# Four-layer graph network on one core: layer 0 with loads two chunks further ahead, its range sums stored from ScalarE's queue into four tables

## The chip, the cores and the metric

The kernel runs on one core of a Trainium2 chip. A core has five engines with instruction queues of their own, TensorE (PE in the profile), VectorE (DVE), ScalarE (ACT), GpSimd (POOL) and SyncE (SP), and sixteen DMA engines that they share. The metric is the device time of one execution in microseconds (us), as the median of several runs without a profiler. The profile is of one further execution.

## What is computed

Four message-passing layers over the same 400,000 edges and 12,500 nodes with 32 features. The edges are sorted by their destination. Every layer starts with a layer normalisation and a relu and adds its result to x:

```python
h = jnp.maximum(_layernorm(x, axis=-1), 0.0)
x = x + _L0_gnn_ref(h, edge_attr_32, L0_gnn_eps, src, dst)
...
def _L0_gnn_ref(node_feat, edge_feat, eps, src, dst):
    m = jax.nn.relu(node_feat[src] + edge_feat)
    neigh = jax.ops.segment_sum(m, dst, num_segments=node_feat.shape[0])
    return (1.0 + eps[0]) * node_feat + neigh
```

Layer 0 thus gathers a row of 32 numbers for each edge, adds that edge's own 32 numbers, applies a relu, and sums by destination. Layers 1 to 3 are of the same form with more work on each edge. Layer 2 needs the degree of each node, the number of edges that leave from it by src; the kernel counts that in layer 0.

## The kernel before

**Tiling.** The edges lie in 128 partitions by 3136 columns (padded). A chunk is 16 columns, 2048 edges; there are 196 chunks. A chunk is worked on in four groups of four columns. Because the edges are sorted by destination, the destinations of a chunk lie in a range of at most 128 nodes; a check at the start confirms that and chooses this "fast" form of all layers.

**The loop.** `edges` (L471 on) is used by layer 0 with all 196 chunks written out in one pass. It runs four groups ahead (`AHEAD`): for group g it fetches group g+4, does the main part of g, and the tail of g-1. The first fetch of a chunk also loads the chunk: `src` (L427, 8 KB), `edge_attr` (L425, 256 KB) and `local` (L408, which holds each edge's place in the chunk's range and, in a last column, the start row of the range). All three are issued by SP, from a pool `big0` of two buffers each. The planner of the framework may move instructions within an engine by its own priorities; it keeps what depends on what.

**A group.** GpSimd issues four indirect DMAs (L433), one for each column, that gather 128 rows of the node features into `hs`; the pool has six `hs` buffers. VectorE adds the edges' numbers (m, L560), ScalarE applies the relu (L561; three m buffers). In the tail, `collect` (L376) makes a one-hot tile `oh` on VectorE (L382) and TensorE adds the messages into the chunk's range in PSUM, `ps_win` (L385). Then the degree count: four small instructions on VectorE for `hi` and `lo` (L575 to L578), two one-hot tiles `ohi` and `olo` (L582), and a product on TensorE into `ps_deg` (L585).

**The end of a chunk.** ScalarE copies `ps_win` to `wsum` (L388, two buffers), and `put` stores that to a table in DRAM from SP's queue (L398), at the start row that SP reads from `local` (L402). Ranges of neighbouring chunks may overlap, so even chunks store to one table and odd ones to another. VectorE adds `ps_deg` to the degrees (L588).

**Before the loop and beside it.** `rest` (L196) is a generator that prepares things: it fills a tile with zeros (L201), clears the tables of all layers with it from ScalarE's queue (`clear`, L313 and L314; 1.6 MB for a table and a small tail), then loads weights and computes unit vectors for later layers. Two steps of it, the two tables of layer 0, are taken before the loop, the others beside its groups.

**After the loop.** `gather_sum` (L363) reads the tables back, by turns on the queues of SP and ScalarE (L369), and VectorE adds them (L372). Then come x and the next layer's normalisation, which everything in layer 1 waits for. Layers 1 and 3 also use two tables, layer 2 four.

**What holds an instruction back.** Each engine takes its instructions in order. A DMA issued by an engine waits, at the head of that engine's queue, for the tiles that it reads or overwrites, and for the transfer that used the same completion semaphore last; eight of these go round over the DMAs of SP and ScalarE. Whatever stands behind it on that engine waits too.

Of the kernel before, what the change touches and what calls it, by code (L numbers as in the profile page):

```python
# [8 lines left out]
F32 = mybir.dt.float32  # L9
# [7 lines left out]
P = 128  # L17
D = 32
# [3 lines left out]
CPI0 = 7  # L22
CPI1 = 196
AHEAD = 4
Q4 = 4
B = G * CG * P // Q4
NTAB = 4
ROUND = 12582912.0

TANH_GAIN = 1.593  # L30
# [5 lines left out]
class GNN:  # L36
# [94 lines left out]
    def weights(self, pool):  # L131
# [19 lines left out]
        nc.vector.memset(hid, 0.0)  # L151
        for q in range(Q4):
            nc.sync.dma_start(hid[32 * q : 32 * q + 10], self.a["w1t"])
# [43 lines left out]
    def rest(self, pool):  # L197

        nc, J = self.nc, self.J
        zero = pool.tile([P, J * D], F32, name="zero")  # L200
        nc.vector.memset(zero, 0.0)  # L201
        for l in range(4):
            for t in self.tabs[l][:2] if self.fast and l != 2 else self.tabs[l]:
                self.clear(t, zero)
                yield
        yield from self.weights(pool)
        if self.fast:
            yield from self.places_by_edge(pool)
            yield from self.unit_vectors(pool)
# [153 lines left out]
    def gather_sum(self, l, pool):  # L363

        nc = self.nc
        parts = []
        for k, t in enumerate(self.tabs[l][: 2 if self.fast and l != 2 else NTAB]):
            s = pool.tile([NP, self.J, D], F32, name=f"part{k}")
            (nc.sync, nc.scalar)[k % 2].dma_start(s.rearrange("p j d -> p (j d)"), self.nodes(t[: self.N]))  # L369
            parts.append(s)  # L370
        for part in parts[1:]:
            nc.vector.tensor_add(parts[0], parts[0], part)  # L372
        return parts[0]


    def collect(self, l, pool, psum, c, feat, t0):  # L376

        nc = self.nc
        if t0 == 0:
            c["sum"] = psum.tile([P, D], F32, name="ps_win")  # L380
        oh = pool.tile([P, G, P], F32, name="oh")
        nc.vector.tensor_tensor(oh, self.iota[:, None, :].to_broadcast([P, G, P]),  # L382
                                c["local"][:, t0 : t0 + G, None].to_broadcast([P, G, P]), op=ALU.is_equal)
        for k in range(G):
            nc.tensor.matmul(c["sum"], lhsT=oh[:, k, :], rhs=feat[:, k, :], start=t0 + k == 0, stop=t0 + k == self.CT - 1)  # L385
        if t0 + G == self.CT:
            s = pool.tile([P, D], F32, name="wsum")
            nc.scalar.copy(s, c["sum"])  # L388
            self.put(l, c, s)

    def get(self, pool, l, c):

# [3 lines left out]
    def put(self, l, c, s):  # L396

        self.nc.sync.dma_start(self.tabs[l][c["no"] % 2][ds(self.first(c), P), :], s)  # L398

    def first(self, c):  # L400
        if "first" not in c:
# [70 lines left out]
    def edges(self, load, gather, front, main, tail, begin=None, windowed=None, beside=None):  # L472


        CPI = CPI1 if self.fast else CPI0
        IT = self.CT * CPI
        with self.tc.For_i(0, self.T // IT, 1) as it:
            i = it * IT
            n = CPI * CG
            chunks, state = {}, {}  # L480
            whole = begin(i) if begin else None

            def fetch(g):
                c, k = divmod(g, CG)
                if k == 0:
                    chunks[c] = load(i + c * self.CT)
                    if whole is not None:
                        chunks[c] |= {x: t[:, c * self.CT : (c + 1) * self.CT] for x, t in whole.items()}
                    chunks[c]["no"] = c
                    if windowed:  # L490
                        windowed(chunks[c], it * CPI + c)
                state[g] = (chunks[c], k * G, gather(chunks[c], k * G))

            def ahead(g):
                state[g] += (front(*state[g]),)

            for g in range(AHEAD):
                fetch(g)
            ahead(0)
            for g in range(n):  # L500
                if g + AHEAD < n:
                    fetch(g + AHEAD)
                if g + 1 < n:
                    ahead(g + 1)
                state[g] = state[g][:2] + (main(*state[g]),)
                if g:
                    tail(*state.pop(g - 1))
                if beside and g > 4 * CG and g % 2:
                    next(beside, None)
            tail(*state.pop(n - 1))  # L510
            for _ in beside or ():
                pass
# [10 lines left out]
    def layer0(self):  # L523
        nc, tc, J = self.nc, self.tc, self.J
# [4 lines left out]
        with ExitStack() as ctx:  # L529
            rest = None  # L530
            if self.fast:
                rest = self.rest(ctx.enter_context(tc.tile_pool(name="rest", bufs=1)))
                for _ in range(2):
                    next(rest)
            big = ctx.enter_context(tc.tile_pool(name="big0", bufs=2))
            gp = ctx.enter_context(tc.tile_pool(name="gather0", bufs=AHEAD + 2))
            wp = ctx.enter_context(tc.tile_pool(name="work0", bufs=2))
            psum = ctx.enter_context(tc.tile_pool(name="psum0", bufs=2, space=PSUM))
            hist = ctx.enter_context(tc.tile_pool(name="hist0", bufs=2, space=PSUM))

            def load(col):
                if self.fast:
                    c = {n: self.load(big, n, col) for n in ("src", "edge_attr_32")}
                else:
                    c = {n: self.load(big, n, col) for n in ("src", "dst", "edge_attr_32")}
                    c["row"] = self.load_row(big, "dst_t", col)
                    c["rows"] = big.tile([P, self.CT], I32, name="rows")
                c["col"] = col
                c["deg"] = hist.tile([P, P], F32, name="ps_deg")
                return c  # L550

            def gather(c, t0):
                return self.gather(gp, "hs", 0, c["src"], t0)

            def front(c, t0, hs):
                return None

            def main(c, t0, hs, _):
                m = wp.tile([P, G, D], F32, name="m", bufs=3)
                nc.vector.tensor_add(m, hs, c["edge_attr_32"][:, t0 : t0 + G, :])  # L560
                nc.scalar.activation(m, m, AF.Relu)  # L561
                return m

            def tail(c, t0, m):
                if self.fast:
                    self.collect(0, wp, psum, c, m, t0)
                else:
                    eq = self.same(wp, c["dst"], c["row"], t0)
                    self.firsts(wp, eq, c["dst"], c["rows"], t0)
                    self.scatter(0, wp, psum, eq, m, c["rows"], t0)  # L570

                hi = wp.tile([P, G], F32, name="hi")
                lo = wp.tile([P, G], F32, name="lo")
                s = c["src"][:, t0 : t0 + G]
                nc.vector.tensor_scalar(hi, s, -0.5 * (J - 1), 1.0 / J, op0=ALU.add, op1=ALU.mult)  # L575
                nc.vector.tensor_scalar_add(hi, hi, ROUND)
                nc.vector.tensor_scalar_add(hi, hi, -ROUND)
                nc.vector.scalar_tensor_tensor(lo, hi, -float(J), s, op0=ALU.mult, op1=ALU.add)  # L578
                ohi = wp.tile([P, G, NP], BF16, name="ohi")
                olo = wp.tile([P, G, J], BF16, name="olo")  # L580
                for oh, v, n in ((ohi, hi, NP), (olo, lo, J)):
                    nc.vector.tensor_tensor(oh, self.iota[:, None, :n].to_broadcast([P, G, n]),  # L582
                                            v[:, :, None].to_broadcast([P, G, n]), op=ALU.is_equal)
                for k in range(G):
                    nc.tensor.matmul(c["deg"][:NP, :J], lhsT=ohi[:, k, :], rhs=olo[:, k, :],  # L585
                                     start=t0 + k == 0, stop=t0 + k == self.CT - 1)
                if t0 + G == self.CT:
                    nc.vector.tensor_add(self.deg, self.deg, c["deg"][:NP, :J])  # L588
                    if not self.fast:
                        nc.scalar.dma_start(self.dst_rows[:, ds(c["col"], self.CT)], c["rows"])  # L590

            self.edges(load, gather, front, main, tail,
                       windowed=(lambda c, row: c.update(self.places_of(big, row))) if self.fast else None, beside=rest)
        with tc.tile_pool(name="end0", bufs=1) as pool:
# [794 lines left out]
```

## Time and profile before

| | us |
|---|---|
| time, median of 3 runs | 19167.42 (19167.29 to 19172.29) |
| the profiled execution | 23109.4 |
| its span in the trace | 23107.7 |
| in it: start, up to the first gather of layer 0 | 0 to 85 |
| layer 0's loop | 85 to 5027 |
| sum of its tables, x, normalisation | 5027 to 5105 |
| layers 1 and 2 | 5105 to 16280 |
| layer 2's end and normalisation | to 16330 |
| layer 3 | 16330 to 23107 |

The profiled execution is longer than the others, so a duration in it is compared with durations in it, and a change of the time with the median.

Layer 0 in the profiled execution, 85 to 5027 us:

| engine | busy us | instructions |
|---|---|---|
| PE | 1831.8 | 9408 |
| DVE | 1975.7 | 6649 |
| ACT | 277.5 | 994 |
| POOL | 3136.3 | 3136 |

A line of groups shows busy time, mean time of one in ns, and the idle time just before such instructions with what ended most of it. A waits line shows who waited for what: the sum, how many times, the longest. A timeline line shows start, length, engine, line and operation; SPq and ACTq are DMA issues on the queues of SP and ScalarE.

### The profile page before, as it was taken

Reading aid. Unit: us, or ns where it says so; the run is one execution under the profiler, and the core shown is the slowest. Engines: PE = TensorE matmul, PEld = TensorE weight load, DVE = VectorE, ACT = ScalarE, POOL = GpSimd, SP = SyncE. Lnnn points to the kernel's source line nnn. Section 1 sums busy time; section 2 is a strip of 40 time slices with the busy share of each in tenths; the row PEclk is TensorE's granted clock in tenths of the full one; section 3 lists DMA queues with packets and bytes.
Section 4 is the critical chain, followed back from the end, with each engine's and each line's share of the span. In section 5 each row is a group of like instructions: output and inputs, shape, how many; then the busy total and the mean of one; then the engine's idle time right before and its main releaser. Section 6 shows DMA issues by size and latency. Waiting matters only on the chain.

```text
span 23107.7 us, 229565 instructions
## 1 busy us (share of the span) xinstructions
PE 15954.9 (69%) x74484; PEld 8493.8 (37%) x74484; DVE 11868.8 (51%) x24410; ACT 5515.5 (24%) x12954; POOL 14407.0 (62%) x12552
## 2 busy tenths in 40 slices
PE   2333333328888778778777777787588888888887
PEld 2333333322333333333333333333355445445544
DVE  4443333335555555555555555555455555555555
ACT  0000000002222222222222222222233333333333
POOL 5666666655777777777777777777444444444443
PEclk9999999998777777777777777777687888888887
DMA  2111111113333333333333333333100000000000
GB/s 74 42 35 23 23 23 23 23 40 73 80 80 79 77 78 83 77 78 82 80 78 81 80 77 79 78 83 77 24 12 12 12 12 12 12 12 12 12 12 18
DMA packets 1503407, 1138.52 MB, mean 49 GB/s; under 512 B 1141492, under 2 KB 1304900, under 8 KB 1448308
## 3 DMA queue, kind: packets, MB, share of 16 engines
q1 hardware_dynamic: 745098, 891.46, 12.3%
q0 software_dynamic: 752640, 206.32, 9.7%
q10 hardware_dynamic: 4448, 25.89, 0.3%
q8 instruction: 592, 9.70, 0.2%
q14 instruction: 629, 5.15, 0.1%
HBM read 1022.56 MB, written 99.86 MB: 49 GB/s over the span
## 4 chain that ended last, share of the span: by engine, by line
PE 39%; DVE 18%; another core or an unknown queue 15%; issue 11%; ACT 9%; POOL 5%; DMA 2%; DVEq 0%; SPq 0%; POOLq 0%; ACTq 0%
PE ps_y L746 11%; PE ps_w L1162 10%; PE ps_o L756 4%; PE ps L879 4%; ACT oh L781 3%; DVE z L749 3%; DVE rb L1180 3%; POOL hs L433 2%; DVE pb L1172 2%; PE ps_h L1140 2%; ACT oh L710 2%; PE ps_win L385 2%; PE ps_sum L1201 1%; DVE f L1178 1%
## 5 line engine op out<-in xcount | busy, mean ns | idle before, releaser
L885 POOL DMA_INDIRECT acc<-summed,rows x3136 | 4995.6, 1593 | 1898.0 <-issue 1141.3
L1130 POOL DMA_INDIRECT hs<-feat,src x3136 | 3085.0, 984 | 3653.4 <-DVE pb L1172 2657.8
L1162 PE MATMUL ps_w<-w2b,hid 128*128 128x256 f32 x12544 | 4006.1, 462 | 608.6 <-issue 430.0
L433 POOL DMA_INDIRECT hs<-feat,src x3136 | 3136.5, 1000 | 1881.0 <-issue 864.2
L704 POOL DMA_INDIRECT hs<-feat,src_c x3136 | 3189.0, 1017 | 1126.7 <-issue 932.0
L1162 PEld LDWEIGHTS ps_w<-w2b,hid 128*128 128x128 f32 x12544 | 2722.3, 227 | 2283.9 <-issue 1572.6
L749 DVE TENSOR_TENSOR z<-ps_y,hid 128x1024 f32<-128x1024 f32 x2352 | 2842.0, 1218 | 1235.5 <-PE ps_y L746 1007.3
L385 PE MATMUL ps_win<-m,oh 128*128 128x32 f32 x6272 | 1488.0, 402 | 2521.3 <-ACT m L561 1829.8
L746 PE MATMUL ps_y<-X,w2t 64*128 64x512 f32 x4704 | 2258.9, 838 | 613.4 <-ACT hid L741 306.4
L385 PEld LDWEIGHTS ps_win<-m,oh 128*128 128x128 f32 x6272 | 1398.1, 328 | 2612.4 <-ACT m L561 1921.6
L1167 DVE TENSOR_TENSOR pa<-ps_w,q 128x512 f32<-128x512 f32 x784 | 536.0, 684 | 3153.4 <-PE ps_w L1162 2928.4
L756 PE MATMUL ps_o<-z,sums 128*32 128x512 f32 x9408 | 1936.9, 697 | 2.5 <-issue 1.6
L746 PE MATMUL ps_y<-Q,w2t 64*128 64x512 f32 x4704 | 1688.5, 740 | 83.6 <-DVE z L749 39.8
L723 PE MATMUL ps_m<-eye,hs 128*32 128x128 f32 x6272 | 805.2, 367 | 1048.3 <-ACT X L729 790.5
L879 PEld LDWEIGHTS ps<-hd,eq 128*128 128x128 f32 x6272 | 1048.0, 253 | 1241.9 <-issue 339.4
L879 PE MATMUL ps<-hd,eq 128*128 128x32 f32 x6272 | 1144.2, 335 | 513.7 <-DVE eq L871 197.1
L732 DVE TENSOR_TENSOR Q<-N,X 128x512 f32<-128x512 f32 x392 | 271.6, 693 | 2115.6 <-ACT X L729 1473.0
L1142 ACT ACTIVATE hid<-ps_h 128x1024 f32<-128x1024 f32 x784 | 799.8, 1020 | 2236.2 <-PE ps_h L1140 1651.5
L1172 DVE TENSOR_TENSOR pb<-ps_w,hs 128x256 f32<-128x256 f32 x3136 | 1281.8, 469 | 0.0
L1140 PE MATMUL ps_h<-emb,w1q 8*128 8x512 f32 x3136 | 1066.5, 761 | 230.0 <-DMA emb<-in_ea_c 165.1
L746 PEld LDWEIGHTS ps_y<-X,w2t 64*128 64x128 f32 x4704 | 603.4, 236 | 1658.0 <-issue 742.6
L723 PEld LDWEIGHTS ps_m<-eye,hs 128*32 128x32 f32 x6272 | 546.2, 147 | 1635.2 <-ACT X L729 929.7
(191 smaller groups left out, 18563.7 us busy)
## 6 DMA issues: line engine op xcount, KB each, us to landing
has<-loc_t SPq DMA_DIRECT2D x392, 1024.0 KB
srow<-in_src_t SPq DMA_DIRECT2D x392, 512.0 KB
hs<-feat,src POOLq DMA_INDIRECT x6272
N<-n_t SPq DMA_DIRECT2D x3136, 32.0 KB
edge_attr<-in_edge_attr SPq DMA_DIRECT2D x196, 256.0 KB
hs<-feat,src_c POOLq DMA_INDIRECT x3136
acc<-summed,rows POOLq DMA_INDIRECT x3136
emb<-in_ea_c SPq DMA_DIRECT2D x784, 20.0 KB
```

The source lines that it names most:

```text
L385: nc.tensor.matmul(c["sum"], lhsT=oh[:, k, :], rhs=feat[:, k, :], start=t0 + k == 0, stop=t0 + k == self.CT - 1)
L433: self.nc.gpsimd.indirect_dma_start(out=t[:, k, :], out_offset=None, in_=self.feats[l][:], in_offset=bass.IndirectOffsetOnAxis(ap=idx[:, t ...
L704: nc.gpsimd.indirect_dma_start(out=c["hs"][:, k, :], out_offset=None, in_=self.feats[1][:], in_offset=bass.IndirectOffsetOnAxis(ap=c["src_ ...
L746: nc.tensor.matmul(y[:, q, :], lhsT=self.w2t[64 * q : 64 * q + 64, j, :], rhs=c["Q" if j < 3 else "X"][64 * q : 64 * q + 64, h, :], start= ...
L749: nc.vector.tensor_mul(z, y, c["hid"][:, 2 * h : 2 * h + 2, :])
L756: nc.tensor.matmul(c["o", j // 3][32 * q : 32 * q + 32, :], lhsT=self.sums[:, j, :], rhs=c["z", j, q // 2][:, q % 2, :], start=j % 3 == 0, ...
L879: nc.tensor.matmul(t[:, k, :], lhsT=c["eq"][:, k, :], rhs=c["hd"][:, G * g + k, :], start=True, stop=True)
L885: nc.gpsimd.indirect_dma_start(out=self.tabs[2][k % NTAB][:], out_offset=bass.IndirectOffsetOnAxis(ap=c["rows"][:, G * g + k : G * g + k + ...
L1130: nc.gpsimd.indirect_dma_start(out=c["hs"][:, k, :], out_offset=None, in_=self.feats[3][:], in_offset=bass.IndirectOffsetOnAxis(ap=c["src" ...
L1140: nc.tensor.matmul(t[:, q, :], lhsT=self.w1q[r : r + 8, m * P : (m + 1) * P], rhs=c["emb"][r : r + 8], start=True, stop=True)
L1162: nc.tensor.matmul(w[:, k, :], lhsT=c["hid"][:, m, 4 * g + k].rearrange("p q s -> p (q s)"), rhs=self.w2b[:, m, :], start=m == 0, stop=m == 1)
L1172: nc.vector.tensor_mul(c["pb"][:, i, gs], w[:, :, lo : lo + 64].rearrange("p g (w u) -> p g w u", u=8), by[:, :, None, :].to_broadcast([P, ...
```

## The change

Layer 0's chunks are asked for two chunks earlier: when the first group of chunk c is fetched, everything up to chunk c+2 that is not yet asked for is loaded (`LEAD`), and `big0` has six buffers instead of two. Its range sums go to four tables by turns instead of two, from four `wsum` buffers instead of two; the start row is read and the store issued on ScalarE's queue instead of SP's (`put_late`). `TABS` says how many tables each layer has; so four tables of layer 0 are cleared ahead of the loop, and four are read and added behind it. The PSUM tile of the degrees is asked for at the chunk's first tail instead of with its loads. Layers 1 to 3 keep their numbers of tables, and the other users of `put` keep it.

```diff
+LEAD = 2
+TABS = {0: 4, 1: 2, 2: 4, 3: 2}
...
-            for t in self.tabs[l][:2] if self.fast and l != 2 else self.tabs[l]:
+            for t in self.tabs[l][: TABS[l]] if self.fast else self.tabs[l]:
                 self.clear(t, zero)
                 yield
...
-        for k, t in enumerate(self.tabs[l][: 2 if self.fast and l != 2 else NTAB]):
+        for k, t in enumerate(self.tabs[l][: TABS[l] if self.fast else NTAB]):
...
         if t0 + G == self.CT:
-            s = pool.tile([P, D], F32, name="wsum")
+            s = pool.tile([P, D], F32, name="wsum", bufs=4)
             nc.scalar.copy(s, c["sum"])
-            self.put(l, c, s)
+            self.put_late(l, c, s)
...
+    def put_late(self, l, c, s):
+
+        first = self.nc.values_load(c["wbase"], engines=[mybir.EngineType.Activation], min_val=0, max_val=self.N - 1)
+        self.nc.scalar.dma_start(self.tabs[l][c["no"] % TABS[l]][ds(first, P), :], s)
...
                 if k == 0:
-                    chunks[c] = load(i + c * self.CT)
-                    if whole is not None:
-                        chunks[c] |= {x: t[:, c * self.CT : (c + 1) * self.CT] for x, t in whole.items()}
-                    chunks[c]["no"] = c
-                    if windowed:
-                        windowed(chunks[c], it * CPI + c)
+                    for c1 in range(len(chunks), min(c + 1 + (LEAD if self.fast else 0), CPI)):
+                        chunks[c1] = load(i + c1 * self.CT)
+                        if whole is not None:
+                            chunks[c1] |= {x: t[:, c1 * self.CT : (c1 + 1) * self.CT] for x, t in whole.items()}
+                        chunks[c1]["no"] = c1
+                        if windowed:
+                            windowed(chunks[c1], it * CPI + c1)
...
-                for _ in range(2):
+                for _ in range(TABS[0]):
                     next(rest)
-            big = ctx.enter_context(tc.tile_pool(name="big0", bufs=2))
+            big = ctx.enter_context(tc.tile_pool(name="big0", bufs=LEAD + 4 if self.fast else 2))
...
-                c["deg"] = hist.tile([P, P], F32, name="ps_deg")
...
+                if t0 == 0:
+                    c["deg"] = hist.tile([P, P], F32, name="ps_deg")
```

## The prediction

> **What bounds the kernel now.** I read the page first, then busy time by stretch, then the waits of layer 0, then the instructions of one pair of chunks, and last the start and the end of layer 0.
>
> From the page (busy us, mean ns of one | idle before, main releaser), and the chain's shares:
>
> ```profile
> span 23107.7 us, 229565 instructions
> ...
> PE 39%; DVE 18%; another core or an unknown queue 15%; issue 11%; ACT 9%; POOL 5%; DMA 2%; DVEq 0%; SPq 0%; POOLq 0%; ACTq 0%
> ...
> L433 POOL DMA_INDIRECT hs<-feat,src x3136 | 3136.5, 1000 | 1881.0 <-issue 864.2
> ```
>
> The profiled execution took 23109.4 us, 3942 us more than the median of 19167.4. Layers 1 to 3 lie after 5027 us, and the change leaves their instructions and order alone but for a few at the border. So only layer 0, 85 to 5027 us, is in play, plus what stands just before and behind it. There POOL issues 3136 gathers, 16 a chunk. One takes 0.94 us and 0.30 us of issue, so a chunk costs 16 x 1.25 = 20.0 us on POOL.
>
> Busy time in four stretches of 500 us (columns: stretch, PE, PEld, DVE, ACT, POOL, clock, DMA share, GB/s):
>
> ```profile
> 500.00:1000.00 500.00, 182.07 (x918) 174.59 (x918) 235.28 (x702) 29.68 (x102) 316.53 (x308) 1.00 0.16 38
> 1500.00:2000.00 500.00, 189.11 (x972) 179.18 (x970) 200.38 (x675) 28.23 (x102) 321.23 (x322) 1.00 0.12 25
> 4000.00:4500.00 500.00, 185.69 (x960) 175.93 (x960) 188.65 (x663) 27.71 (x101) 317.87 (x322) 1.00 0.11 23
> ```
>
> No engine is full. POOL makes 308 to 322 gathers in each stretch, 25 us a chunk instead of 20, and the rate hardly moves while VectorE's load falls from 235 to 189 us. So 5 us a chunk are lost to a wait. The waits of POOL from 2000 to 5000 us (us in total, times, longest):
>
> ```profile
> POOL hs L433 <- issue: 520.7, 1703, 2.1
> POOL hs L433 <- DVE oh L382: 313.4, 35, 14.5
> POOL hs L433 <- DMA src<-in_src: 150.5, 22, 9.4
> ```
>
> One pair of chunks, from the timeline:
>
> ```profile
> 2088.13 0.19 ACT L388 COPY wsum<-ps_win 128x32 f32<-128x32 f32 x1 [22.32 <-remote]
> ...
> 2088.34 0.34 SPq L398 DMA_DIRECT2D acc<-wsum  x1
> 2089.63 0.33 SPq L427 DMA_DIRECT2D src<-in_src  x1
> ...
> 2091.97 0.94 POOL L433 DMA_INDIRECT hs<-feat,src  x1 [7.72 <-DVE oh L382]
> ...
> 2098.43 0.34 SPq L398 DMA_DIRECT2D acc<-wsum  x1
> 2104.79 0.33 SPq L427 DMA_DIRECT2D src<-in_src  x1
> ```
>
> The copy of the range sum waits 22.3 us for a release that the trace can't name. The store of that sum (L398) stands on SP ahead of the next chunk's load of src (L427), so both come late and POOL starts 2.3 us after src is issued. In the next chunk nothing is late: src goes out at 2104.79, while that chunk's 17th gather after 2091.97, the first to need it, is at 2113.40. With 2.3 us for landing, src was 6.3 us early. So the order on SP costs nothing by itself. It costs only when the range sum is late, every second chunk, and what makes it late is the unnamed wait.
>
> **What the Trainium skill says.** "Perfetto Trace Analysis", section "Tensor Engine Instruction (MATMUL, LD_WEIGHTS)", has a matmul's end in a profile as an estimate. So the unnamed 22 us may be TensorE reporting late: matmuls look ended and their results are not released. The trace agrees that far, and does not say whether that happens without the profiler. "DMA: Bandwidth & Descriptors", "Issuing engines are not separate DMA queues", says that transfers of SP and ScalarE run on the same 16 DMA engines; its section "Why a DMA increments its semaphore by 16 and not by 1" splits a transfer over the largest number up to 16 that divides the partitions, five for 125. The trace agrees: two reads of 125x3200 float32, one on each queue, took 26.6 us together, four took 52 (below), so a second queue bought nothing.
>
> **The change, part by part.**
>
> *End: two more tables to sum.* Layer 2 of this kernel already sums four:
>
> ```profile
> 16224.84 14.84 SPq L369 DMA_DIRECT2D part<-acc  x2
> ...
> 16276.84 3.49 DVE L372 TENSOR_TENSOR part<-part,part 125x3200 f32<-125x3200 f32 x1 [0.34 <-DMA part<-acc]
> ```
>
> and layer 0 two:
>
> ```profile
> 5027.16 0.34 SPq L369 DMA_DIRECT2D part<-acc  x1
> ...
> 5053.73 3.49 DVE L372 TENSOR_TENSOR part<-part,part 125x3200 f32<-125x3200 f32 x1 [25.31 <-DMA part<-acc]
> ```
>
> From the first read to the end of the last add: 16280.33 - 16224.84 = 55.5 us against 5057.22 - 5027.16 = 30.1. That is +25.4 us. Of the two added adds (3.49 us each) one or both lie under transfers; if neither did, +29. VectorE waits for nothing else there and layer 1 can't start, so all of it is on the path. I take 25.4, ends 22 and 30.
>
> *Start: two more tables to clear.* The waits of SP at the start, and POOL's first gather and its only long wait for src before 300 us:
>
> ```profile
> SPq L425 <- DMA acc<-zero: 12.2, 1, 12.2
> SPq L408 <- DMA acc<-zero: 9.7, 1, 9.7
> ...
> 84.81 1.47 POOL L433 DMA_INDIRECT hs<-feat,src  x1 [82.96 <-DVE lo L578]
> ...
> POOL hs L433 <- DMA src<-in_src: 14.4, 1, 14.4
> ```
>
> The two waits end at 84.1 and 97.0 us: a clear of 1.6 MB lands every 12.9 us, and loads that share its completion semaphore wait for it. In the changed order four clears stand ahead of the first load. By the instruction order its src waits for the first clear's tail (84.2), the second chunk's src for the third clear (110). With 3 to 9 us to land, the first gather moves from 84.8 to 88 to 94 (+3 to +9), and the second chunk, due 20 us later, waits 2 to 8 more: +5 to +17. Against this stands the 14.4 us wait at the third chunk, whose src came at 130 us behind weight loads on SP. Six chunks are now asked for ahead of the weights, so it goes. Net -9 to +3; I take -2. Three later waits for src (9.3 us from 300 to 1000) go too, some of them into waits for buffers: -4.
>
> *Steady state: loads ahead, and the store on ScalarE's queue.* SP loses per chunk the store (0.34 us) and the reading of its start row (0.95 us between the store's issue and src's at 2089.63); ScalarE gains them, 1.3 us in 20. ScalarE is busy 277.5 of 4942 us in layer 0, and behind the store wait the relus of groups 5 us apart, so this hides; if a relu of each chunk were late by all of it with no slack behind, 196 x 1.3 = 255 us. I take 0: three m and six hs buffers stand between that relu and POOL. The store waits for TensorE (through the copy) as before; queued behind it are now the relus, which also stood behind the copy, and no longer src, local and edge_attr. Four wsum buffers and four tables lengthen the distance between writes to one place; no wait on them shows in the trace, so nothing. The degree tile asked for at the chunk's first tail leaves TensorE's sequence of four and four matmuls as it was.
>
> What the loads ahead save in the middle hangs on the unnamed wait. If it belongs to profiled executions, POOL runs without it at 20 to 21 us a chunk, src is 6 us early, and they save nothing. For this: 15% of the chain, 3466 us, are "unknown", and 3942 us are missing in the runs without a profile. In layer 0 POOL's waits beyond issue are 1881.0 - 864.2 = 1017 us, about a quarter of the missing time, for a stage with a fifth of the span. Against: nothing shows where the missing time lies. I take the saving as 0, ends -208 (all waits for src in layer 0, as the page's trace sums them) and -1017.
>
> Sum, against the profile's own time: +25.4 - 2 - 4 = +19 us, 23109 to 23128, less whatever of the src waits goes there. None of the three terms is a TensorE matter, so I carry them over to the median unchanged: 19167.4 + 19 = 19,186 us.
>
> **Rivals.** Forecast: no measurable change (0.2% of this kernel, 38 us, is what a measurement can tell). The two extra tables eat about what the loads ahead save at the start.
>
> Rival one, faster: the late range sums are real in every execution. Then SP's order stops POOL in every second chunk or so and src, now two chunks ahead, does not. With the waits for src gone and the tables paid: 19167 + 25 - 208 = 18,985. For it: the pair above, where POOL starts 2.3 us after src. Against: from 300 to 1000 us only 9.3 us of src waits, yet the same rate of gathers; there POOL waits for hs buffers held by the same late TensorE, so src waits may only be renamed, and the gain goes towards 0. If POOL's whole idle time went, 19167 + 25 - 1017 = 18,175, the far end.
>
> Rival two, slower: the start is not repaid. Place: ScalarE's queue before 140 us. In the changed order the reading of two start rows stands there ahead of the first relu, and the second row's load waits for the fourth clear, 68 + 16 + 3 x 12.9 = 123 us. The first relu, at 99.9 now, comes at about 125. Six hs groups hold 30 us of gathers from about 90, three m tiles some 15 more. It decides if POOL is stopped by more than about 15 us net; stopped by the full 25, with the 14.4 us saved elsewhere in part, the time is 19167 + 25 + 25 = 19,217.
>
> **How the numbers follow.** No change 0.38; rival one 0.30, and 0.03 for more than that; rival two 0.25, and 0.04 for the store on ScalarE showing (up to 19,440). So faster 0.33, same 0.38, slower 0.29. The forecast's own range is 19,150 to 19,205. To leave out no more than 2 in 10 the range must take rival one to a little below its time and rival two to above it: 18,930 to 19,260.
>
> **What would show it.** Right: first gather at 88 to 94 us; no POOL wait for src after 300 us; the part sum from first read to last add 52 to 60 us; ScalarE's store beside relus that still follow VectorE; layers 1 to 3 as long as before. The steady state is wrong if the median falls below 19,130, the start if the first 16 gathers show waits for hs buffers of over 15 us, ScalarE's share if relus wait for its queue. A profiled layer 0 that is much shorter while the median stays would show that the unnamed wait is the profile's.

## The result and the profile after

The changed kernel takes 19194.3 us in the median of 20 runs (19183.6 to 19214.1), the kernel before, beside it, 19168.0 (19144.5 to 19190.3). The ratio is 1.0015, with an interval of 1.0009 to 1.0022: slower by 17 to 42 us. Most of that interval lies below the 38 us that the prediction called measurable. 19,186 had been forecast.

The page of the changed kernel, the lines that answer to the first ones of before:

```profile
span 19191.0 us, 229975 instructions
...
PE 40%; POOL 22%; DMA 13%; issue 8%; DVE 8%; ACT 8%; another core or an unknown queue 0%; DVEq 0%; POOLq 0%; ACTq 0%; SPq 0%
...
L440 POOL DMA_INDIRECT hs<-feat,src x3136 | 3170.6, 1011 | 1052.0 <-issue 777.1
```

The profiled execution now lasts as long as the others, and the unnamed 15% of the chain are gone. That is no merit of the change: a new profile of the kernel before has none of them either (experiment 1). The first one fits a chip of another kind than that of the times. Experiments 5 to 8 met such a chip, which runs the same program in about 23,200 us with a profiler or without. No record names the chip of that first profile. So before and after are compared below with the profile of experiment 1, and what the change does on the other kind of chip is told apart.

Busy time in three stretches (columns as before):

```profile
500.00:1000.00 500.00, 223.47 (x1104) 212.12 (x1104) 285.53 (x841) 35.79 (x121) 387.85 (x369) 1.00 0.22 48
1500.00:2000.00 500.00, 237.27 (x1164) 228.24 (x1163) 225.93 (x796) 31.44 (x120) 382.42 (x386) 1.00 0.15 27
3500.00:4000.00 500.00, 233.78 (x1148) 225.15 (x1148) 224.00 (x790) 31.29 (x120) 383.58 (x383) 1.00 0.15 27
```

In the last two POOL makes 383 to 386 gathers in 500 us, 1.30 us each: 20.8 us a chunk. The waits of POOL from 300 to 4100 us (total, times, longest):

```profile
POOL hs L440 <- issue: 714.9, 2346, 0.3
POOL hs L440 <- DMA hs<-feat,src: 159.7, 524, 0.3
POOL hs L440 <- DVE hi L586: 4.6, 15, 0.3
```

No single wait is longer than 0.3 us, its own issue time; POOL is the bound of layer 0. A chunk in the middle, from the timeline:

```profile
2094.31 0.17 ACT L390 COPY wsum<-ps_win 128x32 f32<-128x32 f32 x1
2094.51 0.34 ACTq L405 DMA_DIRECT2D acc<-wsum  x1
...
2099.18 0.31 ACT L568 ACTIVATE m<-m 128x128 f32<-128x128 f32 x1 [4.70 <-DVE m L567]
2099.25 0.33 SPq L434 DMA_DIRECT2D src<-in_src  x1
...
2120.48 0.33 SPq L434 DMA_DIRECT2D src<-in_src  x1
```

The store goes out on ScalarE right behind the copy, and the next relu still waits 4.7 us for VectorE, so the store is hidden.

One thing more changed: TensorE's order within a group is turned round. A group of the kernel before (experiment 1), then one of the changed kernel:

```profile
2091.78 1.91 PE L385 MATMUL ps_win<-m,oh 128*128 128x32 f32 x8 [2.72 <-ACT m L561]
2093.50 0.64 PE L585 MATMUL ps_deg<-olo,ohi 128*125 128x100 bf16 x4
...
2095.27 0.56 PE L594 MATMUL ps_deg<-olo,ohi 128*125 128x100 bf16 x4 [2.45 <-DVE olo L591]
2096.03 1.89 PE L387 MATMUL ps_win<-m,oh 128*128 128x32 f32 x8 [0.20 <-DVE hi L584]
```

Before, the range sum comes first and waits for the relu; after, the degree count comes first. All runs with loads ahead (3, 4 and 6 to 12) have the new order, and experiments 1, 2 and 5 the old one. Start and end of the loop:

```profile
84.11 0.33 SPq L434 DMA_DIRECT2D src<-in_src  x1
92.90 1.09 POOL L440 DMA_INDIRECT hs<-feat,src  x1 [91.05 <-DVE hi L584]
...
132.28 0.71 ACT L568 ACTIVATE m<-m 128x128 f32<-128x128 f32 x3 [101.21 <-issue]
...
4235.38 0.67 SPq L371 DMA_DIRECT2D part<-acc  x2
4266.58 3.49 DVE L374 TENSOR_TENSOR part<-part,part 125x3200 f32<-125x3200 f32 x1 [29.95 <-DMA part<-acc]
4289.60 3.49 DVE L374 TENSOR_TENSOR part<-part,part 125x3200 f32<-125x3200 f32 x1 [19.53 <-DMA part<-acc]
4293.01 1.28 DVE L868 TENSOR_SCALAR has<-has,part 128x2048 f32<-128x2048 f32 x1
4294.20 3.49 DVE L374 TENSOR_TENSOR part<-part,part 125x3200 f32<-125x3200 f32 x1
```

The first load waits for the first clear, the first gather comes at 92.9 us. From the first read of a table to the end of the last add it takes 4297.7 - 4235.4 = 62.3 us, against 30.1.

### The profile page after: what moved, and what is told of

It is laid out like the page before. It is cut to its first block, busy times and chain, and to the rows that moved or that the text cites. A ratio compares the mean times of both kernels' runs of the same rounds, so it can differ in the third digit from the quotient of the medians.

```text
span 19191.0 us, 229975 instructions
## 1 busy us (share of the span) xinstructions
PE 14631.1 (76%) x74484; PEld 7969.1 (42%) x74484; DVE 11899.4 (62%) x24412; ACT 5522.6 (29%) x12954; POOL 14592.3 (76%) x12552
## 4 chain that ended last, share of the span: by engine, by line
PE 40%; POOL 22%; DMA 13%; issue 8%; DVE 8%; ACT 8%; another core or an unknown queue 0%; DVEq 0%; POOLq 0%; ACTq 0%; SPq 0%
PE ps_y L755 13%; DMA hs<-feat,src 10%; PE ps_w L1171 10%; POOL hs L440 8%; PE ps_o L765 5%; POOL hs L713 5%; PE ps L888 4%; POOL acc L894 4%; POOL hs L1139 4%; ACT oh L790 3%; DVE z L758 2%; PE ps_h L1149 2%; DVE pb L1181 2%; DMA hs<-feat,src_c 2%; ACT oh L719 2%
## 5 line engine op out<-in xcount | busy, mean ns | idle before, releaser
L713 POOL DMA_INDIRECT hs<-feat,src_c x3136 | 3300.5, 1052 | 1088.9 <-issue 885.4
L1171 PE MATMUL ps_w<-w2b,hid 128*128 128x256 f32 x12544 | 3123.0, 399 | 173.0 <-DVE pb L1181 173.0
L1171 PEld LDWEIGHTS ps_w<-w2b,hid 128*128 128x128 f32 x12544 | 2361.5, 196 | 1174.2 <-issue 499.7
L755 PE MATMUL ps_y<-X,w2t 64*128 64x512 f32 x4704 | 2085.9, 787 | 139.0 <-ACT hid L750 122.6
L755 PE MATMUL ps_y<-Q,w2t 64*128 64x512 f32 x4704 | 1779.7, 772 | 47.1 <-DVE z L758 44.9
L594 PE MATMUL ps_deg<-olo,ohi 128*125 128x100 bf16 x3136 | 444.4, 292 | 1725.3 <-DVE olo L591 1721.5
L567 DVE TENSOR_TENSOR m<-hs,edge_attr 128x128 f32<-128x128 f32 x784 | 237.6, 303 | 2079.1 <-DMA hs<-feat,src 2047.1
L568 ACT ACTIVATE m<-m 128x128 f32<-128x128 f32 x784 | 241.7, 309 | 3747.2 <-DVE m L567 2609.4
L732 PEld LDWEIGHTS ps_m<-eye,hs 128*32 128x32 f32 x6272 | 484.9, 143 | 2008.4 <-ACT X L738 1089.1
L890 ACT COPY summed<-ps 128x128 f32<-128x128 f32 x784 | 207.9, 265 | 3542.9 <-PE ps L888 3161.3
```

The lines of the kernel that those rows point to most:

```text
L713: nc.gpsimd.indirect_dma_start(out=c["hs"][:, k, :], out_offset=None, in_=self.feats[1][:], in_offset=bass.IndirectOffsetOnAxis(ap=c["src_ ...
L732: nc.tensor.matmul(t[64 * q : 64 * q + 32, k * P : (k + 1) * P], lhsT=c["hs"][:, 4 * (2 * h + q) + k, :], rhs=self.eye, start=True, stop=True)
L755: nc.tensor.matmul(y[:, q, :], lhsT=self.w2t[64 * q : 64 * q + 64, j, :], rhs=c["Q" if j < 3 else "X"][64 * q : 64 * q + 64, h, :], start= ...
L1171: nc.tensor.matmul(w[:, k, :], lhsT=c["hid"][:, m, 4 * g + k].rearrange("p q s -> p (q s)"), rhs=self.w2b[:, m, :], start=m == 0, stop=m == 1)
```

## The experiments

Those of one set ran on one chip, beside the kernel before. The sets are 1 to 4, 5 to 8, 9 and 10, 11 and 12. The kernel before took 19,101, 23,199, 19,174 and 19,120 us in them. The first and the third set carry the same chip number, so one kernel can differ by 73 us between two sets; times are compared within a set.

**1. The kernel before, once more.**

> The kernel before, unchanged, profiled once more. Theory A (the unnamed 20 us waits belonged to that one profiled execution): a span near 19,170 us, no long waits of ScalarE's copy for an unnamed release, layer 0's loop from the first gather to the first table read about 4,130 to 4,150 us (20 to 21.2 us a chunk on POOL), src early in every chunk but the third. Theory B (they belong to this kernel's order on SP and went with the change): again a span near 23,100 us with waits of some 20 us in every second chunk. The ratio to the kernel before shows what two equal kernels differ by: within 0.1%.

Measured: 1.0002 (0.9994 to 1.0010). Its page, and POOL's waits up to 300 us:

```profile
span 19106.6 us, 229565 instructions
...
PE 41%; POOL 21%; DMA 13%; DVE 8%; ACT 8%; issue 8%; DVEq 0%; POOLq 0%; SPq 0%; ACTq 0%
...
POOL hs L433 <- DMA src<-in_src: 9.1, 1, 9.1
POOL hs L433 <- DVE hi L577: 8.1, 4, 7.2
```

No unnamed release is in the chain. Its loop takes 4120.6 us from the first gather (85.5) to the first read of a table (4206.1), and after 300 us POOL waits for src 3.3 us in all. So the order on SP cost nothing in the middle here, and 17 us at the start (9.1 + 8.1). The wait of 7.2 us ends at the 33rd gather, the first of the third chunk, whose src went out at 125.9 us behind weight loads; the one of 9.1 us ends at the 81st, the first of the sixth chunk.

**2. Four tables alone.**

```diff
-                for _ in range(2):
+                for _ in range(TABS[0]):
...
-        self.nc.sync.dma_start(self.tabs[l][c["no"] % 2][ds(self.first(c), P), :], s)
+        self.nc.sync.dma_start(self.tabs[l][c["no"] % (TABS[0] if l == 0 else 2)][ds(self.first(c), P), :], s)
```

> The kernel before with layer 0 on four tables, nothing else of the change. Theory A (the tables are the whole cost, at both ends of layer 0): the part sum 25 to 32 us longer, the first gather 3 to 9 us later and the wait at the third chunk still there: +25 to +45 us, more than the whole change (+26). Theory C (the store on ScalarE or the loads cost something, the tables less than that): +10 to +20 us.

Measured: 19158.4 against 19101.0 us, 1.0030 (1.0018 to 1.0042), +57 us (34 to 80): more than the whole change, and above the +25 to +45 of theory A. Its profile has the part sum at 63.5 us and the first gather at 92.9. And POOL waits in the first 300 us:

```profile
POOL hs L434 <- DVE hi L578: 21.4, 2, 21.1
POOL hs L434 <- DMA src<-in_src: 16.7, 2, 11.1
```

That is 38 us of waits instead of 17: 5.6 at the second chunk, 21.1 at the third, whose src now goes out at 149.7 us, and 11.1 at the sixth. +33 at the end, +7 at the first gather and +21 here make +61; the two traces, from their start to the last add, differ by 50.

**3. The change with two tables; 4. loads ahead alone (two tables, the store on SP).**

```diff
-TABS = {0: 4, 1: 2, 2: 4, 3: 2}
+TABS = {0: 2, 1: 2, 2: 4, 3: 2}
...
-            s = pool.tile([P, D], F32, name="wsum", bufs=4)
+            s = pool.tile([P, D], F32, name="wsum")
             nc.scalar.copy(s, c["sum"])
-            self.put_late(l, c, s)
+            self.put(l, c, s)
```

(Experiment 3 has the first hunk, experiment 4 both, each against the changed kernel. So "loads ahead alone", here and in 9 and 11, keeps the later degree tile and TensorE's new order.)

> The changed kernel with two tables in layer 0: loads ahead and the store on ScalarE's queue stay. Theory A: the saving at the start alone, the 14 us wait for src at the third chunk gone: -15 to 0 us against the kernel before, layer 0's loop otherwise as long. Theory B (loads ahead save waits in the steady state): -100 us or more. Theory C (the store on ScalarE is paid in every chunk): +20 us or more.

> Loads two chunks ahead in six buffers alone; two tables, the store on SP's queue. Theory A: -15 to 0 us, the same as with the store on ScalarE's queue. Theory B (the store ahead of src on SP is what holds src, so that loads ahead help only with both): 0 here, -20 or more with the store moved too.

Measured: 0.9998 (0.9990 to 1.0007) and 1.0003 (0.9994 to 1.0011). Neither can be told from the kernel before here. In both traces no wait for src is left in the first 300 us. With experiment 2 this shows the tables as the change's cost, and that the rest, with the store moved or not, costs or brings no more than about 20 us on this chip.

**5. The store on ScalarE's queue alone; 6. the change once more.** For 5:

```diff
-            self.put(l, c, s)
+            self.put_late(l, c, s)
...
+        first = self.nc.values_load(c["wbase"], engines=[mybir.EngineType.Activation], min_val=0, max_val=self.N - 1)
+        self.nc.scalar.dma_start(self.tabs[l][c["no"] % 2][ds(first, P), :], s)
```

> The store of the range sum and the reading of its start row on ScalarE's queue alone; two tables, loads as before. Theory A: nothing, within 8 us, the wait for src at the third chunk as before. Theory C (each store costs something on the path): +20 us or more, with POOL's mean step between gathers larger in all of layer 0.

> The changed kernel once more, beside the runs of its parts. Theory A: first gather 7 us later, the waits of about 19 us in the first chunks down to 5, the part sum 32 us longer: +26 us (10 to 40), so that tables alone (+57) and loads ahead alone (about 0) do not add up, because loads ahead cover most of what the clears do to the first chunks. Theory E (the parts add up): +50 us or more.

This set met a chip on which 27 runs of the kernel before took 23119 to 23294 us. Measured there: the store alone 1.0010 (0.9996 to 1.0023), and the whole change 0.9882 (0.9863 to 0.9902), 22938 against 23199: 261 us faster. Neither theory had that. POOL's waits in layer 0 after 300 us, first with the store alone, then with the change, and the copy's unnamed waits of the change:

```profile
POOL hs L438 <- DVE oh L382: 537.0, 49, 15.7
POOL hs L438 <- DVE ohi L587: 113.9, 10, 21.8
POOL hs L438 <- DMA src<-in_src: 83.4, 14, 15.3
```

```profile
POOL hs L440 <- DVE lo L587: 286.8, 112, 7.4
POOL hs L440 <- DMA hs<-feat,src: 32.0, 105, 0.3
POOL hs L440 <- DVE m L567: 17.7, 9, 5.0
...
ACT wsum L390 <- remote: 558.4, 41, 37.2
```

The trace names TensorE after all: in the changed kernel's loop every unnamed wait ends with an update of the one semaphore that only TensorE's instructions update. The late releases are not fewer. In 61 of the 196 chunks the copy starts over 3 us after the modelled end of its last matmul, up to 36 us; with the store alone in 63, in experiment 1 in 6.

What is gone after 300 us is every wait of POOL for src, and its long waits for hs buffers. The loop takes 4653.9 us, with the store alone 4989.3 (4942.4 in the first profile of before). Waits for src can be only the smaller part of these 335 us: with the store alone they are 83 us in all. The larger part goes with VectorE. The two largest of its unnamed waits from 300 us to near the loop's end, with the store alone and with the change:

```profile
DVE deg L593 <- remote: 884.2, 66, 30.6
DVE oh L382 <- remote: 663.6, 85, 27.2
```

```profile
DVE deg L597 <- remote: 602.7, 43, 31.7
DVE m L567 <- remote: 352.0, 28, 29.7
```

With the store alone VectorE stops 85 times at a new one-hot tile, until TensorE has released an old one, and the adds that free hs buffers stand behind that. With the change no such stop is left. So it takes something beside the store: the loads ahead with their six buffers, the later degree tile with TensorE's new order, or the four wsum buffers. Four tables are not needed, since experiment 8 has two and a loop of 4679.3 us. No run on this chip has one of these without the others, and whether the store must move too is open as well: experiments 9, 11 and 12 would have told that, and met chips of the other kind.

**7. The change with each table read in three pieces; 8. two tables, and all transfers of 125 partitions in such pieces.**

```diff
-            (nc.sync, nc.scalar)[k % 2].dma_start(s.rearrange("p j d -> p (j d)"), self.nodes(t[: self.N]))
+            for a, b in ((0, 96), (96, 124), (124, 125)):
+                (nc.sync, nc.scalar)[k % 2].dma_start(s[a:b].rearrange("p j d -> p (j d)"), self.nodes(t[: self.N])[a:b])
```

> The changed kernel with each table read back as three transfers of 96, 28 and 1 partitions instead of one of 125, in all layers. Theory D (the part sums are bound by the five DMA engines that one transfer of 125 partitions runs on): layer 0's sum falls from 62 to 20 to 30 us, the ten table reads of the four layers together give 80 to 110 us back against the changed kernel. Rival (memory or the loads queued behind the reads bound it): 20 us or less.

> Loads ahead and the store on ScalarE's queue with two tables, and every transfer of 125 partitions (table reads and clears, x, the features, the result) in the three pieces of 96, 28 and 1. Theory D: 100 to 170 us faster than the kernel before, with the first gather some 20 us earlier because x and the clears land sooner. Rival: 40 us or less.

Measured on that chip: 22881 and 22813 us, 0.9852 (0.9836 to 0.9868) and 0.9835 (0.9815 to 0.9855). Experiment 7 gains 57 us on the changed kernel, less than theory D and more than its rival, and the sum of four tables takes 42.5 us instead of 62.3, not 20 to 30. The pieces help; what limits them is not shown. Experiment 8 is 125 us faster than the changed kernel, two tables and pieces together; its 386 us against the kernel before hold the gain of loads ahead on this chip, which its forecast did not have.

**9. Loads ahead alone again; 10. experiment 8 again.**

> Loads two chunks ahead alone, two tables, the store on SP's queue, tried again for the kind of chip it runs on. Where the kernel before takes about 23,200 us (late releases of TensorE in every second chunk): Theory F (loads ahead are the whole gain there, the store may stay on SP): -300 us, the changed kernel's -261 plus the 33 us of its end and some of its start. Rival (the store must leave SP too, since src stands behind it): -100 us or less. Where the kernel before takes about 19,100 us: 0 again.

> Loads ahead and the store on ScalarE's queue with two tables, and all transfers of 125 partitions in pieces of 96, 28 and 1. Where the kernel before takes about 19,100 us: theory D 80 to 130 us faster (0.4 to 0.7%), all of it at the start and at the ends of the layers; rival 20 us or less. Where it takes about 23,200 us: -390 us as before.

The chip was of the first kind. Loads ahead: 0.9989 (0.9982 to 0.9995), 29 us faster. Experiment 10: 19099 against 19174 us, 0.9961 (0.9947 to 0.9974), 75 us faster, a little below what was expected. Its end of layer 0, two tables in three pieces each:

```profile
4233.48 1.08 SPq L375 DMA_DIRECT2D part<-acc  x3
...
4250.78 3.49 DVE L378 TENSOR_TENSOR part<-part,part 125x3200 f32<-125x3200 f32 x1 [16.05 <-DMA src_c<-in_src_c]
4254.31 3.49 DVE L609 TENSOR_TENSOR x<-x,part 125x3200 f32<-125x3200 f32 x1
```

4254.3 - 4233.5 = 20.8 us instead of 30.2. The first gather comes at 80.8 us, 5 us earlier and not 20. Where the rest of the 75 us lies was not traced. This version beats the kernel before on both kinds of chip, and the changed kernel where that ran beside it (experiment 8).

**11. Loads ahead alone; 12. with the store on ScalarE, two tables.**

> As e9: loads ahead alone, the store on SP. On a chip where the kernel before takes about 23,200 us: Theory F -300 us; rival (src still stands behind the late store on SP) -100 us or less. On a chip where it takes about 19,100 us: -30 to +5 us.

> Loads ahead and the store on ScalarE's queue, two tables. On a chip where the kernel before takes about 23,200 us: Theory F the same as e11 within 30 us; rival 200 us less than e11. On a chip where it takes about 19,100 us: within 15 us of e11.

Both 0.9991 (0.9985 to 0.9998), 19103 and 19106 against 19120 us. With experiment 9 that makes loads ahead, with or without the store, worth 15 to 29 us in three of five readings and nothing that can be told in two; the 17 us of waits that they take from the start are of that size. The store makes no difference on these chips.

## Why the prediction was right, and where it was not

*The sum.* +19 us was forecast, +26 measured. The terms, with what the changed kernel's trace and experiment 1 show:

| term | forecast | measured |
|---|---|---|
| end: two more tables to sum | +25.4 (22 to 30) | +32.1 |
| start: first gather later | +3 to +9 | +7.4 (85.5 to 92.9) |
| start: second chunk waits for src | +2 to +8 | +5.8 |
| waits that go, at the start and up to 1000 us | -14.4 - 4 | -17.2 |
| steady state | 0 | no new wait; its length is not resolved |

32.1 + 7.4 + 5.8 - 17.2 = +28. That is a sum of parts of two traces from different sets. From their start to the last add the traces themselves differ by 4297.7 - 4236.3 = 61.4 us, so the loop's middle is 33 us longer in the changed kernel's trace. No wait of POOL accounts for that, and loops differ as much between sets: loads ahead alone took 4114.1, 4140.8 and 4094.6 us from the first gather to the first read in experiments 4, 9 and 11. So the close fit of the sum to +26 says little about the middle.

*The term that was mis-sized is the end.* The forecast took layer 2's sum of four tables as the pattern, where one add was left after the last transfer. In layer 0 the transfers alone took 4289.6 - 4235.4 = 54.2 us against 26.7, which is +27.5. Then two adds stood behind them, not one, and the planner had put a piece of layer 1's preparation (L868, 1.28 us) between these: +4.6 more. The prediction's bound of both adds in the open (+29) left out the piece of layer 1 and the 2.2 us by which four transfers took longer than in layer 2; the measured +32.1 lies beyond it and beyond the stated end of 30.

*The start* came as the instruction order gave it: load for load behind the clears that share its semaphore. The waits that go were misread, though. The 14.4 us in the profile of before are at the 81st gather (224.8 us), the sixth chunk; the third chunk's wait, to which the prediction gave them, is another one, of 13.4 us, shown there as a wait for VectorE. With the new profile the two are 9.1 and 7.2 us, and the waits from 300 to 1000 us, priced at 4, are not there. That -18.4 met -17.2 is luck in part.

Rival two's place is real: the first relu came at 132.3 us, later than the 125 forecast. Yet POOL was not stopped by it. That is 39 us after the first gather, and the prediction counted hs and m buffers for about 45. In experiment 2, whose first relu came at 111.9, POOL was stopped for 38 us by another thing, src that comes late, most of all behind the weight loads. The parts do not add up for that reason: loads ahead ask for the third chunk before the weights, and are worth more beside four clears than beside two.

*The steady state* was forecast at 0 because src is early in an undisturbed chunk and the store on ScalarE is hidden. Experiment 1's 3.3 us of waits for src in the middle show the first, experiment 12 beside 11 the second. The prediction had TensorE's sequence as it was, with the later degree tile; in the changed kernel it is turned round (the two groups above). It is so in experiment 4 too, so neither the tables nor the store do that. On a chip of the quicker kind it cost nothing that could be told.

*The reason given for it was wrong.* The prediction read the 3942 us between profile and median as a cost of the profiled execution. They go with a kind of chip: the unprofiled runs of experiments 5 to 8 show the same 23,200 us. The forecast for the median held because the median came from a chip of the other kind, which is luck. Where TensorE's releases are late, the time goes rival one's way: -261 us, 78 more than the 183 us that it priced from the waits for src alone. Its mechanism, src behind the late store on SP, is not what showed: taking the store off SP brought nothing in experiment 5, whose trace has fewer waits for src than the profile of before (83 us instead of 193) and more for hs buffers. What shrank with the change is mostly the waits for hs buffers, behind VectorE. The test that the prediction named, a shorter profiled layer 0 with the same median, could not tell a profile from a chip.

## What to carry to other kernels

Before a wait in a profile is priced against a median, ask whether both come from the same conditions: a profiled execution 20% longer than the median may have been on a different chip, and then every wait in it is evidence for that chip alone. A change that brings nothing on one chip may be worth 1% on one where an engine reports late, so it needs its measurement on both. An edit that only asks for a buffer later can turn an engine's order round: compare the order of every engine in the two traces before a part of a change is called alone. More tables cost their clears and reads at the two ends of a stage, in the open, and buy nothing unless a wait on them can be shown in between.

## What the runs showed of the hardware

Two kinds of chip run the same program 21% apart (19,101 and 23,199 us, each steady within 1% over 34 and 27 runs). In layer 0 the clock granted to TensorE was 1.00 on both, so the clock is not the cause there. What shows is that a copy of TensorE's result starts up to 36 us after the modelled end of its last matmul (experiment 6), on the semaphore of TensorE. Whether the matmuls ran late or were only reported late is not shown. In layer 3 the clock was 0.96 on the quicker chip (experiment 1) and 0.80 on the other. The cause stays open.

A transfer of 125 partitions in pieces of 96, 28 and 1 was quicker than in one piece: two tables 20.8 instead of 30.2 us. The Trainium skill, "DMA: Bandwidth & Descriptors", "Why a DMA increments its semaphore by 16 and not by 1", gives, by its rule of the largest divisor up to 16, five DMA engines for 125 partitions and sixteen and fourteen for 96 and 28; the direction agrees, the gain is less than the number of engines would give. No run here shows how many engines a transfer used.
